# Where TensorE's sums over the states stand in a scan step: ahead of the step's middle third or behind it

## The chip, the core and the metric

The kernel runs on one core of a Trainium2 chip, as one program. The metric is the time of one execution on the device in microseconds. The core's engines run at the same time, each from a queue of its own that it works through in order: TensorE (PE in the profile) multiplies matrices, VectorE (DVE) does elementwise work, reductions and scans, ScalarE (ACT) activations and copies, GpSimd (POOL) a few copies and the indirect transfers, and SyncE (SP) starts most transfers between the device's memory and the core's.

## The reference

The reference is one decoder layer in float32 over 8 sequences of 512 tokens with 512 features: a state-space block (Mamba), cross attention, and a layer of 32 experts, with a layer norm behind each. The part that the change touches is the scan of the first block:

```python
dt = jax.nn.softplus(dt @ dt_proj_w + dt_proj_b)
dA = jnp.exp(A[None, None] * dt[..., None])
dBx = dt[..., None] * B_ssm[:, :, None, :] * x_main[..., None]

def scan_fn(h, inp):
    dA_t, dBx_t, C_t = inp
    h = dA_t * h + dBx_t
    y_t = jnp.einsum('bdn,bn->bd', h, C_t)
    return (h, y_t)
...
y = y + x_main * D_param[None, None, :]
y = y * jax.nn.silu(z)
out = res_scale * (y @ out_proj_w) + residual
```

There are 1024 channels with 16 states each. `einsum('bdn,bn->bd')` is the sum over the states: the states `h` times `C`, added up over the 16 states of a channel.

## The kernel before

The kernel has three phases: `layers` (scan, attention, router and the shared expert), `experts` and `finish`. Only `layers` matters here. It goes over 16 chunks: 8 sequences of two halves with 256 tokens each. A chunk has 32 steps, `k` = 0 to 31, one for each of four quarters `q` of the channels, four groups `g` of the states, and two halves `jj` of a quarter. A step works on a tile `h` of 128 partitions (32 channels with 4 states each) by 4 by 257 values. There are six such tiles in turn (L487).

One step, in the order in which the source emits it:

- `steps_in` (L494, VectorE) multiplies the repeated `dt*x` (tile `rep`) by `B` (tile `bc`) into `h`. In a step with `k` mod 8 = 1, `gated` (L535, VectorE) also multiplies the finished `py` of the quarter before into `zs`.
- the first third of the step's parts;
- `scan` (L501, VectorE) runs the recurrence over `h` with the decays `l_da`;
- for the next step, `carry` (L488, ScalarE) takes a new `h` and puts the old state into it, and `decays` (L480, ScalarE) forms its exponentials in one of two tiles `l_da`; then `keep` (L506, ScalarE) saves the state of the step before;
- the middle third of the parts;
- the sums over the states of the pair of steps before, if there are any: `products` (L519 and L521, TensorE);
- `collect` (L510, VectorE) multiplies `h` by `C`, and every second step it makes the next `products`;
- the last third of the parts.

`products` of the steps `k` = 2p and 2p + 1 is made at the end of step 2p + 1 and emitted in step 2p + 2, so it is emitted in even steps. Four matmuls, one for each 32 rows of the accumulator `py` in PSUM, add up the states of both `h` of the pair with the constant `fold`; at the first group of a quarter one more (L519) starts `py` with `x*D`. There is one `py`. In the profile each of these matmuls counts as two instructions. When they are done, both `h` are free again.

The "parts" are everything else that has to go on beside the scan. `part` puts them on a list, and the list is split into thirds by place (L1154 to L1156): the rest of the chunk's own projection (`gate_x` and `convolve`, L343 in the profile, 16 instructions each), `prepare` (L437: the `dt` of the next quarter), `back` (L552: the projection out, in two calls of 16 instructions, followed by `norm`, L561), and, by a budget of weights, the units of the attention of the sequence before (`units`) and the keys and values of the next one (`sources`; their matmuls are L756). In the attention `maximum` (L819 on TensorE, then L821 on VectorE) finds the largest score, `negate` (L828) turns the four maxima of a pair of heads into rows, `weigh` (L845, then L849 on ScalarE) takes the exponentials of the scores, and `gather` (L861) multiplies them by the values. One budget covers two chunks: an even chunk begins with the next sequence's keys and values and comes to the attention near its step 18; the odd chunk behind it ends the attention near its step 15 and then does the router and the shared expert. The chunks 0 and 1 have no attention, since there is no sequence before them.

In which third a part lands follows from how many there are: of one part it is the middle third, of two none is in the middle, of three one, of four two, of five one. So at `k` = 2 the middle third of a chunk without other work is `back`, at `k` = 4 `gate_x`; in the last even steps of an even chunk and the first of an odd one it is, for example, `weigh` and `gather`, or `weigh`, `gather` and `negate`.

The order of the source is not yet the order in an engine's queue: a scheduler between the two lays out the queues, and it can let an instruction that is ready pass one that is not. The waits between the engines, and for a free buffer, are then made from the data that instructions share.

Of the kernel before, what the change touches and what calls it, by code (L numbers as in the profile page):

```python
# [89 lines left out]
def layers(ctx, tc, a, x1d, filld, based, xbuf, arm):  # L90
# [203 lines left out]
    def settle(force=False):  # L294

        due, later = [], []
        for x in left:
            (due if force or not clock or x[0] <= clock[0] else later).append(x)
        for _, part in due:
            rest = part()  # L300
            if rest:
                later.append(rest if isinstance(rest, tuple) else (0, rest))
        left[:] = later
        return due
# [107 lines left out]
    def bcast(f, g):  # L412

        got = []
        for r0 in (g, NST + g):
            t = bcp.tile([P, T], F32, tag="bc", name="bc")
            src = f["scr"].rearrange("(n s g) t -> n g s t", n=2, s=NQ)[r0 // NST, r0 % NST]
            nc.sync.dma_start(t, src.unsqueeze(0).to_broadcast([QP, NQ, T]))
            got.append(t.unsqueeze(1).to_broadcast([P, NB, T]))
        f["bc", g] = got  # L420
# [63 lines left out]
    def carry(t, q, g, jj):  # L484

        last = state[:, q, g, jj].unsqueeze(2)
        h = mp.tile([P, NB, T + 1], F32, tag="h", name="h", bufs=6)  # L487
        nc.scalar.copy(h[:, :, 0:1], last if t else nothing)  # L488
        return h
# [217 lines left out]
    def sources(b):  # L707

        st, todo = {}, []

        def begin():
            load("Wv")
            st["cT"] = cT = quad("s2", "cT")
            nc.sync.dma_start(cT, rows(a["ctx"][b]))
            st["mk"] = mk = p1.tile([P, S], U8, tag="mk", name="mk")
            nc.sync.dma_start(mk, a["mask"][b : b + 1, :].to_broadcast([P, S]))
            kept[b] = [dp.tile([S, D], F32, tag="vd", name="vd"), dp.tile([D, S], F32, tag="kd", name="kd")]

        def values(pc):
            if pc == 0:  # L720
                load("Wk")
            w, cT = loaded["Wv"], st["cT"]
            ps = dense(lambda dc: cT[:, dc, pc * P : (pc + 1) * P], lambda dc: w[:, dc, :])

            def put():
                v = p3.tile([P, D], F32, tag="row", name="v")
                nc.scalar.copy(v, ps)
                nc.sync.dma_start(kept[b][0][pc * P : (pc + 1) * P, :], v)

            return put  # L730

        def keys(oc):
            if oc == 0 and b:
                load("Wq")
            w, cT = loaded["Wk"], st["cT"]
            ps = dense(lambda dc: w[:, dc, oc * P : (oc + 1) * P], lambda dc: cT[:, dc, :])

            def put():

                k = p3.tile([P, D], F32, tag="row", name="k")  # L740
                nc.vector.scalar_tensor_tensor(k, ps, bk[:, oc : oc + 1], st["mk"], ALU.add, ALU.mult)
                nc.sync.dma_start(kept[b][1][oc * P : (oc + 1) * P, :], k)

            return put

        todo.append((0, begin, False))
        for j in range(SC):
            todo.append((3.4, lambda j=j: values(j), False))
        for j in range(DC):
            todo.append((3.4, lambda j=j: keys(j), False))  # L750
        return todo
# [307 lines left out]
    def do(fn, *args, first=False):  # L1059

        if first:
            dry(False)
        rest = fn(*args)
        settle()
        if rest:
            left.append(rest if isinstance(rest, tuple) else (0, rest))
# [6 lines left out]
    def work(k):  # L1073

        front = 6.9 if k in (2, 3) else 3.4 if 4 <= k < 8 or k in (12, 14, 17, 20, 23) else 1.0 if k in (11, 25) else 0.0
        return 1.2 + front
# [24 lines left out]
    ahead, products = carry(0, 0, 0, 0), None  # L1101
# [3 lines left out]
    for i, (b, t) in enumerate(chunks):  # L1105
        nf = {}
        after = chunks[i + 1] if i + 1 < len(chunks) else None
        if t == 0:
            side, spent = units(b - 1) if b else sources(0), 0.0

            own = [work(k) for k in range(len(steps))] * 2
            whole = sum(own) + sum(x[0] for x in side)
        for k, (q, g, jj) in enumerate(steps):
            if i and k == 1:
                bcast(f, NG - 1)
            if after and 28 <= k < 31:
                bcast(nf, k - 28)
            qf, nq = (f, q + 1) if q + 1 < CC // 2 else (nf, 0)
            h = ahead

            parts = []

            def part(fn, *args, first=False):
                parts.append((do, fn, *args, first))

            if k in (2, 3) and old:
                part(back, k - 2, *old)
            if 4 <= k < 8:
                part(gate_x, k - 4, f)
            if k == 8:  # L1130
                parts.append((finish_silu, f["zs"]))
            if k % 8 == 0 and q + 1 < CC // 2:
                part(prepare, q + 1, f)
            if k == 25 and after:
                part(prepare, 0, nf)
            if after:
                if k == 8:
                    part(norm_x, nf)
                if k == 11:
                    for j in range(DC // 2):  # L1140
                        part(flip_x, j, nf)
                if k in (12, 14, 17, 20):
                    part(convolve, after[1], (12, 14, 17, 20).index(k), nf, first=(k == 12))
                if k == 22:
                    parts.append((finish_silu, *nf["xs"].values()))
                if k == 23:
                    part(x_proj, nf)
            if side and (k >= 4 or t and k < 2):
                at = t * len(steps) + k + 1
                while side and spent + sum(own[:at]) <= whole * at / len(own):  # L1150
                    w, fn, alone = side.pop(0)
                    spent += w
                    part(fn, first=alone)
            thirds = [[], [], []]  # L1154
            for m, x in enumerate(parts):
                thirds[round((m + 0.5) * 3 / len(parts) - 0.5) if x[0] is do else 1].append(x)  # L1156

            def run(m):
                clock[0] += 1
                settle()  # L1160
                for x in thirds[m]:
                    if x[0] is do:
                        do(*x[1:-1], first=x[-1])
                    else:
                        x[0](*x[1:])

            steps_in(f, q, g, jj, h)
            more = qf is f or after
            if k % 8 == 6 and more:
                repeat(qf, nq, 0, 1)  # L1170
            if k % 8 == 1:
                if k > 1:
                    gated(q - 1, f)
                elif old:
                    gated(CC // 2 - 1, old[2])
            if i == 0 and k == 0:
                load("Wo")
            if i == 0 and k == 2:
                biases()
            if k == 0 and old:  # L1180
                twice_x(*old)
            if k == 5 and after:
                load_x(*after, nf)
            run(0)
            scan(das[n % 2], h)
            n += 1

            if k + 1 < len(steps) or after:
                then = steps[(k + 1) % len(steps)]
                ahead = carry(t if k + 1 < len(steps) else after[1], *then)  # L1190
                decays(f if k + 1 < len(steps) else nf, *then, das[n % 2])
                if k % 8 == 5 and more:
                    repeat(qf, nq, 0, 0)
                    repeat(qf, nq, 1, 0)
                if k % 8 == 6 and more:
                    repeat(qf, nq, 1, 1)
            if held:
                keep(*held)
            held = t, q, g, jj, h
            run(1)  # L1200

            if products:
                products()
            products = collect(f, q, g, jj, h)
            run(2)
            while i < 2 and cleared < E * (i * len(steps) + k - 6) // (2 * len(steps) - 7):
                clear(cleared)
                cleared += 1
        while t and side:
            _, fn, alone = side.pop(0)  # L1210
            do(fn, first=alone)
        old = (b, t, f)
        f = nf
# [435 lines left out]
```

## Time and profile before

Three runs took 5262.2, 5269.8 and 5275.3 us; the median is 5269.8 us.

| what | us |
| --- | --- |
| the profiled execution | 5265.2 |
| its span, first to last instruction | 5263.4 |
| PE busy | 4483.6 (85%) |
| DVE busy | 4170.1 (79%) |
| ACT busy | 2584.7 (49%) |
| `scan` L501, 512 of 2.29 | 1165.1 |
| `collect` L510, 512 of 1.22 | 618.6 |
| `steps_in` L494, 512 of 1.22 | 613.9 |
| sums L521, 2048 instructions | 370.8 |
| sums L519, 128 instructions | 77.6 |
| ACT's `carry` (L488) waiting for the sums, 74 times | 111.3 |
| PE waiting for the maximum L821 at L819, 94 times | 139.4 |
| PE waiting for the maximum L821 at `negate` (L828), 34 times | 74.8 |

A line of a group gives the line of the code, the engine, the operation and its tiles; then, behind a bar, the time that the group was busy and the mean duration of one in ns; then, behind another bar, how long the engine was idle just before these instructions, and what ended most of that. A line of a timeline has the start, the busy time and the instruction; `x2` says that two equal neighbours were merged, and the bracket gives the idle time before and what ended it. PE's four matmuls of one sum run beside each other on 32 columns each, so eight instructions of some 0.6 us take 1.06 us together.

### The profile page before, as it was taken

The page shows a single profiled execution, that of the slowest core. Times are in us where ns is not written, and L with a number is a line of the kernel's source. Part 1 is how long each engine was busy: PE and PEld are TensorE (multiplying, and loading weights), DVE is VectorE, ACT ScalarE, POOL GpSimd, SP SyncE. Part 2 cuts the span into 40 slices and gives each one's busy share as a digit, 9 for nine tenths or more (in the row PEclk, how much of TensorE's full clock was granted, in tenths as well). Part 3 has the DMA queues.
Part 4 walks back from the last instruction along what each step waited for, and adds up shares of the span by engine and source line. Part 5 has one row for each costly group of instructions (what it writes and reads, how often), then busy time and mean ns, then how long its engine had stood idle before and what let it go on. Part 6 is the DMA issues. An engine that isn't in the chain of part 4 may idle for free. (4 is left out here: it accounts for less than half of the span.)

```text
span 5263.4 us, 54340 instructions
## 1 busy us (share of the span) xinstructions
PE 4483.6 (85%) x17184; PEld 2454.6 (47%) x17184; DVE 4170.1 (79%) x5333; ACT 2584.7 (49%) x5765; POOL 587.0 (11%) x426
## 2 busy tenths in 40 slices
PE   6768879888888988888898888878899999999895
PEld 3324234333423423343342343333478888877775
DVE  7999898989989998998999899883356666655555
ACT  5566565655556556565656656543222333323233
POOL 1000002001100200200020020010112111111111
PEclk8879999999998999999898999989899999999998
DMA  8885345435634634543473454433244444444344
GB/s 236 265 231 156 74 118 175 116 97 135 180 83 104 200 95 107 161 142 97 95 217 74 120 176 116 107 106 106 96 116 134 133 126 134 134 124 126 116 125 157
DMA packets 486437, 711.62 MB, mean 135 GB/s; under 512 B 121576, under 2 KB 205064, under 8 KB 483952
## 3 DMA queue, kind: packets, MB, share of 16 engines
q1 hardware_dynamic: 449984, 626.90, 41.8%
q0 software_dynamic: 33280, 67.81, 5.8%
q10 hardware_dynamic: 2736, 11.54, 0.5%
q8 instruction: 220, 3.60, 0.3%
q14 instruction: 217, 1.78, 0.1%
HBM read 391.24 MB, written 164.79 MB: 106 GB/s over the span
## 5 line engine op out<-in xcount | busy, mean ns | idle before, releaser
L480 ACT ACTIVATE l_da<-rep,l_aneg 128x256 f32<-128x256 f32 x2048 | 893.4, 499 | 948.1 <-DVE h L501 884.5
L501 DVE TENSOR_TENSOR_SCAN h<-l_da,h 128x1028 f32<-128x1028 f32 x512 | 1165.1, 2290 | 20.9 <-ACT l_da L480 18.3
L494 DVE TENSOR_TENSOR h<-rep,bc 128x1024 f32<-128x1024 f32 x512 | 613.9, 1216 | 107.7 <-PE py L521 90.7
L510 DVE TENSOR_TENSOR h<-h,bc 128x1024 f32<-128x1024 f32 x512 | 618.6, 1215 | 2.0
L521 PE MATMUL py<-h,l_fold 128*32 128x512 f32 x2048 | 370.8, 647 | 110.1 <-DVE h L510 92.3
L819 PE MATMUL ps_s<-l_ka,l_qa 64*128 64x512 f32 x1024 | 329.2, 714 | 139.8 <-DVE mx L821 139.4
L1334 PE MATMUL ps_h<-xT,w 128*128 128x224 f32 (+3 forms) x1536 | 376.4, 395 | 36.8 <-issue 29.7
L1427 POOL DMA_INDIRECT based<-y,xe x160 | 272.8, 1705 | 1157.8 <-ACT y L1406 432.4
L821 DVE TENSOR_REDUCE mx<-ps_s 128x2 f32<-128x1024 f32 x256 | 310.0, 1216 | 66.5 <-PE ps_s L819 66.2
L861 PE MATMUL po<-eT,l_va 128*64 128x512 f32 x1024 | 303.6, 674 | 47.5 <-ACT eT L849 42.9
L1334 PEld LDWEIGHTS ps_h<-xT,w 128*128 128x128 f32 x1536 | 293.3, 192 | 100.3 <-issue 41.6
L845 PE MATMUL ps_t<-l_qa,l_ka 64*128 64x512 f32 x1024 | 306.0, 669 | 23.9 <-ACT eT L849 23.3
L849 ACT ACTIVATE eT<-ps_t 128x1024 f32<-128x1024 f32 x256 | 258.7, 1015 | 128.7 <-PE ps_t L845 128.5
L694 POOL DMA_INDIRECT xbuf<-x2t,dest x128 | 217.2, 1697 | 863.2 <-DVE dest L679 762.4
L343 PE MATMUL ps_z<-xnT,wm 128*128 128x256 f32 x1024 | 237.7, 388 | 28.7 <-DVE o L561 23.7
L756 PE MATMUL ps_p<-x2T,wa 128*128 128x512 f32 x512 | 242.0, 627 | 20.5 <-ACT hT L950 13.8
L552 PE MATMUL po<-wm,zs 128*128 128x512 f32 x512 | 246.7, 636 | 13.4 <-DVE z L963 11.7
L1334 PE MATMUL ps_h<-t,s 128*128 128x224 f32 (+3 forms) x1024 | 247.4, 392 | 5.8 <-DVE hT L1355 5.8
L343 PE MATMUL ps_x<-xnT,wm 128*128 128x256 f32 x1024 | 245.6, 392 | 4.9 <-ACT xnT L332 2.8
L1355 DVE TENSOR_TENSOR hT<-ps_h,p 128x224 f32<-128x224 f32 (+3 forms) x128 | 55.3, 432 | 242.7 <-PE ps_h L1334 242.7
L343 PEld LDWEIGHTS ps_z<-xnT,wm 128*128 128x128 f32 x1024 | 194.9, 193 | 90.5 <-DVE o L561 37.0
L343 PEld LDWEIGHTS ps_x<-xnT,wm 128*128 128x128 f32 x1024 | 195.5, 195 | 81.6 <-issue 44.8
(239 smaller groups left out, 6971.3 us busy)
## 6 DMA issues: line engine op xcount, KB each, us to landing
w<-in_w SPq DMA_DIRECT2D x93, 1024.0 KB
wm<-in_in_proj_w SPq DMA_DIRECT2D x128, 512.0 KB
rep<-dt SPq DMA_DIRECT2D x256, 256.0 KB
rep<-dtx SPq DMA_DIRECT2D x256, 256.0 KB
xbuf<-zero SPq DMA_DIRECT2D x32, 1362.5 KB
xe<-xbuf SPq DMA_DIRECT2D x32, 1362.5 KB
wm<-in_out_proj_w SPq DMA_DIRECT2D x64, 512.0 KB
wa<-in_sw SPq DMA_DIRECT2D x24, 1024.0 KB
```

The costliest lines, as they stand in the source:

```text
L343: nc.tensor.matmul(ps[:, i, :], w[:, dc, i * P : (i + 1) * P], f["xnT"][:, dc, :], start=(dc == 0), stop=(dc == DC - 1),)
L480: nc.scalar.activation(da[:, n, 1:], dt[:, j, i, :], AF.Exp, scale=aneg[:, 2 * q + i, 2 * jj + j, g : g + 1])
L494: nc.vector.tensor_tensor(h[:, :, 1:], dtx.rearrange("p j i t -> p (j i) t"), f["bc", g][0], ALU.mult)
L501: nc.vector.tensor_tensor_scan(flat, da.rearrange("p n t -> p (n t)"), flat, 0.0, ALU.mult, ALU.add)
L510: nc.vector.tensor_tensor(h[:, :, 0:T], h[:, :, 1:], f["bc", g][1], ALU.mult)
L521: nc.tensor.matmul(f["py"][j * QP : (j + 1) * QP, :, :], fold, hs[j // 2][:, 2 * (j % 2) : 2 * (j % 2) + 2, 0:T], start=False, stop=g == N ...
L819: nc.tensor.matmul(ps[:, j, :], qa[r, lt * P : (lt + 1) * P], ka[r, :], start=True, stop=True)
L821: return lambda: nc.vector.tensor_reduce(mx[:, lt, :].unsqueeze(2), ps, AX.X, ALU.max) and None
L845: nc.tensor.matmul(ps[:, j, :], ka[r, kc * P : (kc + 1) * P], qa[r, :], start=True, stop=True)
L861: nc.tensor.matmul(po[j * 2 * HD : (j + 1) * 2 * HD, :], va[:, kc, i, j * HD : (j + 2) * HD], eT[:, j, :], start=(kc == 0), stop=(kc == SC ...
L1334: nc.tensor.matmul(ps, w[:, n, r * P : (r + 1) * P], x[:, n, 0:cols], start=not more and n == 0, stop=n == 1, skip_group_check=more,)
L1427: put = nc.gpsimd.indirect_dma_start(out=based, out_offset=bass.IndirectOffsetOnAxis(ap=xe.bitcast(I32)[:, j, D + E :], axis=0), in_=ys[j] ...
```

## The change

The sums of the pair before are emitted directly behind the next scan and what ScalarE does for the step, and the middle third of the parts comes behind them. The sums themselves, the parts, and how these are split into thirds stay as they were.

```diff
             if held:
                 keep(*held)
             held = t, q, g, jj, h
-            run(1)
-
             if products:
                 products()
+            run(1)
+
             products = collect(f, q, g, jj, h)
             run(2)
```

## The prediction

> **What bounds the kernel now.** I read the table by stretches first, then the groups by line, then the waits, and last the timelines of VectorE (DVE) and TensorE (PE).
>
> By stretches (start:end, length, then busy time of each engine, granted clock and DMA):
>
> ```profile
> 820.00:1000.00 180.00, 158.09 (x535) 73.39 (x533) 166.19 (x180) 101.54 (x245) 38.10 (x21) 0.97 0.61 178
> 1000.00:1097.00 97.00, 77.13 (x298) 23.44 (x298) 85.68 (x71) 54.83 (x120) 0.00 (x0) 0.89 0.28 62
> 1097.00:1139.00 42.00, 39.83 (x152) 20.95 (x150) 35.83 (x39) 17.95 (x44) 0.00 (x0) 0.98 0.55 166
> 820.00:1275.00 455.00, 382.20 (x1383) 165.61 (x1381) 411.56 (x452) 267.05 (x595) 41.24 (x29) 0.94 0.47 129
> ```
>
> The last line is two chunks, one batch. DVE is busy 411.6 of 455 us (90%), PE 382.2 (84%). Neither covers the batch alone: in the attention (1000 to 1097) DVE idles 11.3 us and PE 19.9, in turns; from 1097 to 1139 PE is all but full (39.8 of 42). The experts start near 3500 us and are not touched.
>
> The groups on the path, from the page, and DVE's wait on the sums from the list of waits:
>
> ```profile
> L494 DVE TENSOR_TENSOR h<-rep,bc 128x1024 f32<-128x1024 f32 x512 | 613.9, 1216 | 107.7 <-PE py L521 90.7
> L521 PE MATMUL py<-h,l_fold 128*32 128x512 f32 x2048 | 370.8, 647 | 110.1 <-DVE h L510 92.3
> ```
>
> ```profile
> DVE h L494 <- PE py L521: 90.7, 38, 6.8
> ```
>
> So 38 times `steps_in` (L494) waited for the sums (L521) to give back a buffer of `h`. There are six buffers, three pairs of steps, and L494 of one pair waits for the sums of the pair three before it. The sums stand far back in PE's queue: near 1505 us they run 35 us after the `collect` that they need. The reverse wait, sums for collect, is 92.3 us, and 60.2 of it lie before 350 us.
>
> Where the 90.7 us are, DVE and PE of one batch:
>
> ```profile
> 1053.05 2.36 DVE L494 TENSOR_TENSOR h<-rep,bc 128x1024 f32<-128x1024 f32 x2 [2.54 <-PE py L521]
> ...
> 1069.36 2.36 DVE L494 TENSOR_TENSOR h<-rep,bc 128x1024 f32<-128x1024 f32 x2 [3.28 <-PE py L521]
> ...
> 1107.24 2.36 DVE L494 TENSOR_TENSOR h<-rep,bc 128x1024 f32<-128x1024 f32 x2 [5.42 <-PE py L521]
> ```
>
> ```profile
> 1063.25 0.27 PE L828 MATMUL ps_m<-l_ident,mx 128*2 128x128 f32 x1 [3.23 <-DVE mx L821]
> 1063.46 1.35 PE L819 MATMUL ps_s<-l_ka,l_qa 64*128 64x512 f32 x4
> 1064.41 2.02 PE L845 MATMUL ps_t<-l_qa,l_ka 64*128 64x512 f32 x4
> 1066.36 1.97 PE L861 MATMUL po<-eT,l_va 128*64 128x512 f32 x4
> 1068.26 1.07 PE L521 MATMUL py<-h,l_fold 128*32 128x512 f32 x8
> ```
>
> ```profile
> 1097.56 7.78 PE L552 MATMUL po<-wm,zs 128*128 128x512 f32 x16
> 1105.18 1.02 PE L519 MATMUL py<-xs,l_ident 128*128 128x512 f32 x2
> 1106.13 1.06 PE L521 MATMUL py<-h,l_fold 128*32 128x512 f32 x8
> ...
> 1115.83 3.72 PE L343 MATMUL ps_z<-xnT,wm 128*128 128x256 f32 x16 [1.56 <-DVE o L561]
> ```
>
> At 1053 to 1069 there is a ring: the sums free `h`, DVE runs two L494 (2.36 us), a maximum (1.22), two scans (4.48), a collect (1.20) and a maximum (1.22); PE, which idled 3.23 us for that maximum, runs `negate`, `maximum`, `weigh`, `gather`, and only then the next sums. The round took 16.3 us (1053.05 to 1069.36), and the middle third of that step is `weigh` and `gather`: they stand between the transposes and the sums.
>
> **The change part by part.** Nothing is added or removed; the 256 groups of sums (8 matmuls, 1.06 us; every fourth with two of L519, 1.02 us) move ahead of the middle third of an even step. They issue no DMA. What they pass, by which part falls in that third: `weigh`, `gather`, `negate`, some `maximum` (about 1.1 us each), `gate_x` and `convolve` (3.7 us), `back` (7.8 us), `prepare` (1.1 us), and in others nothing on PE. SP's queue keeps its issues; the loads that such a part starts are only issued behind it as before. POOL's and ACT's work is not passed, only PE's.
>
> Source order is not queue order: two L494 stand ahead of two scans at 1053, though each step writes L494, scan, collect. At 1139 `negate` ran ahead of a `gather` written before it. So not-ready work was overtaken when the queues were laid out, and I expect a sum to pass a ready part only where its collects are done by that layout's time.
>
> Now the waits of L494, read one by one from DVE's timeline in the seven odd chunks that carry attention (3 to 15).
> - Step 0: 1.10, 2.54, 2.67, 2.48, 2.64, 1.18, 1.09, in all 13.7 us. The sums pass `weigh` and `gather`, 1.92 + 1.22 = 3.1 us at 1049 to 1052: more than any of the waits. All 13.7 go.
> - Step 2: 2.35, 3.28, 3.17, 3.22, 3.19, 3.22, 3.15, in all 21.6 us. They pass 2.02 + 1.97 = 4.0 us: all 21.6 go. By the ring: 16.3 less 4.0 is 12.3 us, less than DVE's own work in it, 12.5 us (16.3 less its idle 3.28 and 0.53), so DVE then sets the pace.
> - The last quarter of the even chunk, step 28: seven times 1.29, 9.0 us. They pass one `gather` at 1.0 us: 7.0 go.
> - Step 6: 6.82, 5.42, 5.34, 5.36, 5.35, 5.36, 5.34, in all 39.0 us. The sums pass `back` (7.8 us), so this wait too ends. But PE works without a break from 1097.56 to 1114, and `norm` (L561) waits for the end of both `back` calls, which is the same in either order. What DVE gains it mostly spends waiting for L561. What remains is the 1.56 us that PE idles for L561 ahead of `gate_x`, into which the next sums (1.06) now fall. I take 7 x 1.06 = 7.4; the bounds are 0 and 39.0.
> - The other seven or so waits, 90.7 - 13.7 - 21.6 - 9.0 - 39.0 = 7.4 us: at step 20 the middle third has no PE work. Nothing goes.
>
> The cost: what is passed comes 1.06 us later. In PE's slack that is free: 19.9 us per batch in the attention, and in the first chunks PE waits for DVE anyway. It is not free for `prepare` at step 8 of an even chunk, which stands right ahead of its sums (901.99, then 903.05) and for which DVE waits 3.10 us (L457 at 913.34). There 7 x 1.07 = 7.5 us are lost. If PE's slack were gone, each of the 197 even steps that have PE work in their middle third would cost up to 1.06 us; bounds 0 and 209, and I take the 7.5, near the lower, since the table by stretches shows 84% for PE.
>
> Sum: -13.7 - 21.6 - 7.0 - 7.4 + 7.5 = -42.2 us. The profiled span of 5263.4 becomes 5221; with the 1.8 us around it (5265.2 - 5263.4) 5223. That execution was 4.6 us under the median shown (5269.8), so **5228 us**.
>
> A rule on the clock bears on the ring. In the rows, after 3.23 us of idling `weigh` and `gather` took 2.02 and 1.97 us; after the 0.66 us idle ahead of the next round they took 1.02 and 1.08. The Trainium skill, "TensorE: Matmul & The Clock Gate" (The HAM clock gate), says an idle window of about 3.4 us halves the clock and about as long a busy one restores it. By it, idling cut from 3.2 to under 1 us would also give back the 1.8 us of each round; that lies within the waits counted above, so the sum is not changed.
>
> A rule against the change: "PSUM — Partial Sum Buffer" (Engine vs sequencer instructions) says matmuls start and complete in program order. The row agrees: PE idled 92.3 us at L521 for collects, nothing passing. By the rule alone every late sum now also holds the part it has passed; what that would make is the third rival.
>
> **The rivals.**
> - *The waits only move.* The freed DVE meets the maximum's scores (L821 waits 66.2 us for L819 now) or `rep` (the decays wait 53.7 us) instead. For it: step 6 is just such a case. Against: in the ring DVE's and PE's work both fit in 14 us. It gives nothing back but the 7.5 lost at most: about 5270.
> - *All of it comes.* If `norm` does not hold DVE at step 6, 90.7 us go: 5269.8 - 90.7 = 5179. Against: PE's full stretch.
> - *PE is held in order* (the slower side). Place: chunks 0 to 2, where DVE is behind PE. There nine even steps per chunk have `prepare`, `back`, `gate_x` or `convolve` in the middle third. If the sums are queued ahead of these though their collects are late, PE stands for the mean wait seen there, 60.2 / 17 = 3.5 us, with 1 to 8 us of work behind it. 27 x 3.5 = 95 us, of which DVE feels what delays `convolve` and `prepare`. It decides from 12 of the 27 on, when it eats the 42 us. In full: 5270 + 95 - 42 = 5323; half: 5275 to 5290. For it: the 92.3 us and the strict order. Against: the layout overtakes late work, and in these chunks PE has room.
>
> **How the numbers follow.** The forecast 0.48, all of it 0.10, the waits only move 0.17, PE held 0.25. What this kernel's measurement can tell from no change is 0.3%, 16 us: the forecast and "all of it" are faster, 0.58; the moved waits are the same, 0.17; PE held is slower, 0.25. The forecast's own range is 5190 (most of step 6 too) to 5250 (half of the ring). With the rivals 5180 to 5295: the low end takes most of the 90.7, the high end the half-held case and a little more.
>
> **What would show it.** L494's wait for PE falls from 90.7 us to 30 or less, with none over 4 us at step 2; `weigh` and `gather` near 1064 to 1068 stand behind the sums; PE's wait for the maximum (139.4 us, and 74.8 at `negate`) shrinks; the batch's period falls from 455 us by about 6. Wrong: L494's wait goes and DVE's idle time at L821, L457 or L561 grows as much; or PE's wait at L521 for L510 rises well over 92 us before 700 us, and the first two chunks get longer.

## The result and the profile after

| kernel | median us | lowest to highest | runs |
| --- | --- | --- | --- |
| before | 5266.0 | 5260.5 to 5275.3 | 4 |
| after | 5311.6 | 5305.5 to 5318.1 | 4 |

The ratio is 1.0089, with a 95% interval of 1.0077 to 1.0102: the change made the kernel 46 us slower, where 42 us less were forecast. The profiled execution took 5316.9 us, with a span of 5315.2.

The two groups that the change is about, from the page of after:

```profile
L494 DVE TENSOR_TENSOR h<-rep,bc 128x1024 f32<-128x1024 f32 x512 | 612.0, 1213 | 77.8 <-PE py L521 59.5
L521 PE MATMUL py<-h,l_fold 128*32 128x512 f32 x2048 | 396.5, 668 | 109.8 <-DVE h L510 96.4
```

VectorE's (DVE's) list of waits of after (who waits for whom: total us, times, longest):

```profile
DVE mx L821 <- PE ps_s L819: 139.2, 67, 10.2
DVE h L494 <- PE py L521: 59.5, 32, 3.5
...
DVE st L62 <- DMA xt<-in_x: 39.3, 7, 6.0
...
DVE o L561 <- PE po L552: 31.3, 8, 12.0
```

And TensorE's (PE's):

```profile
PE ps_t L845 <- DVE mx L821: 40.4, 7, 5.8
...
PE ps_z L343 <- ACT v L727: 15.2, 6, 3.4
```

The wait that the change aimed at did fall, 90.7 to 59.5 us. Other waits more than took its place: the maximum waits for its scores (L821, 66.2 to 139.2), the first operation on the next chunk's input for its load (L62, 5.7 to 39.3), `norm` for `back` (L561, 11.3 to 31.3); on PE two waits are new, 40.4 us at L845 (before 0.5) and 15.2 at L343 for ScalarE's (ACT's) copy L727 (before none).

**Where the 46 us are.** I took the start of every scan in both traces and subtracted the lengths of the same step pairs (pair 6 is the time from the scan of step 6 to that of step 8). The first two chunks are 1.5 us longer in all. In chunks 2 to 15 the steps 6 to 11 of the even chunks lose 48.5 us (8.5, 26.6 and 13.4 by pair). In the odd chunks step 4 gains 18.9 and step 6 gives back 11.6, and the pairs 10 and 12 go by -58.4 and +76.9, a net loss of 18.5. Not all of this stays: the steps 12 to 17 of the even chunks give 10.5 back, and over all their steps the even chunks lose 37.6 us and the odd ones 9.5. The even chunks are read best from the table by stretches, taken from the scan of step 2 to that of step 12 of the chunks 4 to 14, six rows for each kernel (the first and the sum are shown; the columns are start:end, length, busy time of PE, its weight loads, DVE, ACT and POOL, PE's granted clock, DMA share, GB/s). Before:

```profile
846.50:916.30 69.80, 63.84 (x213) 31.04 (x211) 58.92 (x65) 38.37 (x96) 21.20 (x12) 0.98 0.71 225
...
sum 417.10, PE 383.60 PEld 186.51 DVE 353.71 ACT 230.36 POOL 127.38; mean PE 63.93 PEld 31.09 DVE 58.95 ACT 38.39 POOL 21.23
```

After:

```profile
853.00:928.00 75.00, 66.99 (x216) 32.36 (x216) 58.73 (x66) 39.22 (x98) 18.30 (x11) 0.93 0.65 206
...
sum 463.70, PE 404.98 PEld 193.34 DVE 352.66 ACT 235.12 POOL 134.35; mean PE 67.50 PEld 32.22 DVE 58.78 ACT 39.19 POOL 22.39
```

These stretches alone are 46.6 us longer. PE was busy in 92% of them before: it is the engine nearest to its limit there, though over a batch it has 16% to spare. DVE's work is the same. PE's idle time grew by 25.2 us (46.6 - 21.4), and its busy time by 21.4, for nearly the same number of matmuls (216 against 213 in the row shown), at a granted clock of 0.91 to 0.96 where it had 0.98.

**What happens there**, in chunk 4. In the even chunk's step 4 the sums pass one block of `values` (L756, 3.7 us), `h` comes free earlier, and the layout of DVE's queue now has inputs and scans ready while `norm` goes through its five short dependent operations, L74 to L79. It puts them between. DVE's timeline before:

```profile
882.94 0.16 DVE L74 TENSOR_TENSOR m<-v,r 128x2 f32<-128x2 f32 x1 [3.23 <-ACT r L70]
...
883.73 0.16 DVE L79 SCALAR_TENSOR_TENSOR less<-mv,r 128x2 f32<-128x2 f32 x1
```

After:

```profile
889.13 0.16 DVE L74 TENSOR_TENSOR m<-v,r 128x2 f32<-128x2 f32 x1 [3.23 <-ACT r L70]
889.24 1.23 DVE L494 TENSOR_TENSOR h<-rep,bc 128x1024 f32<-128x1024 f32 x1
...
891.81 2.29 DVE L501 TENSOR_TENSOR_SCAN h<-l_da,h 128x1028 f32<-128x1028 f32 x1
894.02 0.13 DVE L77 TENSOR_TENSOR r<-r,m 128x2 f32<-128x2 f32 x1
894.07 2.29 DVE L501 TENSOR_TENSOR_SCAN h<-l_da,h 128x1028 f32<-128x1028 f32 x1
896.28 0.13 DVE L79 SCALAR_TENSOR_TENSOR less<-mv,r 128x2 f32<-128x2 f32 x1
...
904.33 1.29 DVE L62 BATCH_NORM_STATS2 st<-xt 128x6 f32<-128x512 f32 x2 [5.64 <-DMA xt<-in_x]
```

From the start of L74 to that of L79 it is 7.15 us instead of 0.79. ACT waits for L79, and what stands behind that wait is late too. ACT's timeline after:

```profile
894.13 1.30 ACT L480 ACTIVATE l_da<-rep,l_aneg 128x256 f32<-128x256 f32 x3 [3.69 <-DVE h L501]
896.45 1.52 ACT L81 ACTIVATE o<-o,less,r 128x512 f32<-128x512 f32 x2 [1.01 <-DVE less L79]
897.88 0.49 ACT L480 ACTIVATE l_da<-rep,l_aneg 128x256 f32<-128x256 f32 x1
898.27 0.56 ACT L727 COPY v<-ps_p 128x512 f32<-128x512 f32 x1
```

ACT's first wait, 3.69 us, is for a scan that gives the decays their buffer back. The wait for L79 and the two L81 behind it then put 2.5 us more (1.01 + 1.52) ahead of the copy L727. L727 empties the PSUM bank of a `values` block whose matmuls ended near 893.2 (in the kernel before this copy ran at 888.86), and PE waits for it ahead of the third `gate_x`. PE's timeline before:

```profile
886.91 7.07 PE L343 MATMUL ps_z<-xnT,wm 128*128 128x256 f32 x32
```

After:

```profile
893.10 3.62 PE L343 MATMUL ps_z<-xnT,wm 128*128 128x256 f32 x16
898.89 5.41 PE L343 MATMUL ps_z<-xnT,wm 128*128 128x256 f32 x16 [2.18 <-ACT v L727]
```

Before, these 32 matmuls ran in one piece of 7.07 us. Now PE waits 2.18 us, and the sixteen behind the wait take 5.41 us instead of 3.62: 4 us in a stretch where PE has little to spare.

### The profile page after: what moved, and what is told of

It is laid out like the page before. It is cut to its first block, busy times and chain, and to the rows that moved or that the text cites. A ratio compares the mean times of both kernels' runs of the same rounds, so it can differ in the third digit from the quotient of the medians.

```text
span 5315.2 us, 54319 instructions
## 1 busy us (share of the span) xinstructions
PE 4541.0 (85%) x17184; PEld 2467.2 (46%) x17184; DVE 4160.0 (78%) x5333; ACT 2595.7 (49%) x5765; POOL 599.0 (11%) x426
## 5 line engine op out<-in xcount | busy, mean ns | idle before, releaser
L494 DVE TENSOR_TENSOR h<-rep,bc 128x1024 f32<-128x1024 f32 x512 | 612.0, 1213 | 77.8 <-PE py L521 59.5
L510 DVE TENSOR_TENSOR h<-h,bc 128x1024 f32<-128x1024 f32 x512 | 616.2, 1214 | 1.8
L521 PE MATMUL py<-h,l_fold 128*32 128x512 f32 x2048 | 396.5, 668 | 109.8 <-DVE h L510 96.4
L819 PE MATMUL ps_s<-l_ka,l_qa 64*128 64x512 f32 x1024 | 348.3, 719 | 164.4 <-DVE mx L821 164.3
L821 DVE TENSOR_REDUCE mx<-ps_s 128x2 f32<-128x1024 f32 x256 | 309.6, 1214 | 139.3 <-PE ps_s L819 139.2
L845 PE MATMUL ps_t<-l_qa,l_ka 64*128 64x512 f32 x1024 | 325.3, 690 | 54.1 <-DVE mx L821 40.4
L861 PE MATMUL po<-eT,l_va 128*64 128x512 f32 x1024 | 298.3, 663 | 30.4 <-ACT eT L849 23.4
L343 PE MATMUL ps_z<-xnT,wm 128*128 128x256 f32 x1024 | 239.1, 390 | 25.2 <-ACT v L727 15.2
L819 PEld LDWEIGHTS ps_s<-l_ka,l_qa 64*128 64x128 f32 x1024 | 95.4, 206 | 353.3 <-DVE mx L821 268.9
L756 PE MATMUL ps_p<-x2T,wa 128*128 128x512 f32 x512 | 241.4, 626 | 18.4 <-ACT hT L950 12.5
L552 PE MATMUL po<-wm,zs 128*128 128x512 f32 x512 | 235.2, 613 | 24.0 <-DVE z L963 20.2
L343 PE MATMUL ps_x<-xnT,wm 128*128 128x256 f32 x1024 | 248.5, 396 | 7.1 <-ACT xp L363 6.1
L343 PEld LDWEIGHTS ps_x<-xnT,wm 128*128 128x128 f32 x1024 | 198.5, 198 | 82.1 <-issue 40.9
```

Of the source, the lines that this page charges most:

```text
L343: nc.tensor.matmul(ps[:, i, :], w[:, dc, i * P : (i + 1) * P], f["xnT"][:, dc, :], start=(dc == 0), stop=(dc == DC - 1),)
L494: nc.vector.tensor_tensor(h[:, :, 1:], dtx.rearrange("p j i t -> p (j i) t"), f["bc", g][0], ALU.mult)
L510: nc.vector.tensor_tensor(h[:, :, 0:T], h[:, :, 1:], f["bc", g][1], ALU.mult)
L521: nc.tensor.matmul(f["py"][j * QP : (j + 1) * QP, :, :], fold, hs[j // 2][:, 2 * (j % 2) : 2 * (j % 2) + 2, 0:T], start=False, stop=g == N ...
L819: nc.tensor.matmul(ps[:, j, :], qa[r, lt * P : (lt + 1) * P], ka[r, :], start=True, stop=True)
L821: return lambda: nc.vector.tensor_reduce(mx[:, lt, :].unsqueeze(2), ps, AX.X, ALU.max) and None
```

## The experiments

All keep the computation. "Early" is the changed place of the sums, "late" that of the kernel before. In e1, e2, e3 and e15 one condition chooses, with `i` the chunk and `k` the step:

```diff
+            early = bool(products and CONDITION) and (products() or True)
             run(1)
-            if products:
+            if products and not early:
                 products()
```

Most of the others lay one instruction behind another in its engine's queue (`tc.issue_after`); nothing else about the instruction changes.

| kernel | median us | ratio to before | interval |
| --- | --- | --- | --- |
| e1_all_but_step4 | 5279.8 | 1.0029 | 1.0018 to 1.0041 |
| e2_step4_alone | 5287.4 | 1.0041 | 1.0028 to 1.0053 |
| e3_attention_alone | 5266.2 | 1.0001 | 0.9992 to 1.0010 |
| e4_norm_held | 5305.0 | 1.0076 | 1.0061 to 1.0091 |
| e6a_maximum_spread | 5229.9 | 0.9931 | 0.9918 to 0.9945 |
| e6b_maximum_first | 5255.5 | 0.9988 | 0.9978 to 0.9997 |
| e8_own_buffer | 5320.8 | 1.0112 | 1.0096 to 1.0128 |
| e8c_own_buffer_before | 5272.0 | 1.0014 | 1.0004 to 1.0023 |
| e9_spread_alone | 5238.2 | 0.9934 | 0.9922 to 0.9947 |
| e10_copies_first | 5291.9 | 1.0045 | 1.0033 to 1.0057 |
| e11_step4_copies_first | 5286.7 | 1.0039 | 1.0026 to 1.0052 |
| e12_step4_norm_whole | 5272.1 | 1.0018 | 1.0009 to 1.0027 |
| e13_norm_whole | 5288.5 | 1.0052 | 1.0033 to 1.0071 |
| e14_norm_whole_spread | 5260.7 | 0.9992 | 0.9984 to 1.0001 |
| e15_two_places_back | 5248.2 | 0.9974 | 0.9965 to 0.9984 |
| e16_two_places_back_spread | 5220.6 | 0.9923 | 0.9909 to 0.9936 |

The kernel before, run beside them, had medians from 5262.7 to 5270.0 us; so ratios are compared, not medians.

### Which steps lose

```diff
+ e1: CONDITION = not (i % 2 == 0 and k == 4)
+ e2: CONDITION = (i % 2 == 0 and k == 4)
```

> The sums are early as in the changed kernel, except those of step 4 of every even chunk, which stay behind the middle third there (one group of 16 per even chunk, 8 groups of 256). Theory (norm torn apart): with step 4's sums early, h is free early, and VectorE's queue is laid out with two L494 and two scans between the five small operations of norm (L74 to L79), so o is stored and xt loaded some 7 us late; steps 6 to 10 of the even chunks 4 to 14 cost 48 us in all. Then this kernel gives back 35 to 50 of the 46 us: 5262 to 5277, VectorE's wait at L62 for xt under 10 us. Rival (the new waits are spread: VectorE waits for the scores at L821, 87 us against 13): still 5300 to 5312.

> The kernel before, with the sums early at step 4 of every even chunk alone. Theory (norm torn apart): this one move makes nearly all of the loss: 5300 to 5315, VectorE waiting 30 us or more at L62 for xt, L494's wait for the sums as before (80 to 91 us). Rival (spread): 7 groups of 256 moved, within 5 us of before, about 5266 to 5271.

Taking one of the 32 sums of a batch back (e1) returns 0.0089 - 0.0029 = 0.6%, 32 of the 46 us; that one alone (e2) costs 0.41%, 22 us. Both times lie between the two ranges that were expected: the place is right in both directions, but it is not nearly all of the loss. That it costs less alone than its return brings, by 10 us, is within the intervals. A second place was then read from the profiles, the pairs 10 and 12 of odd chunks. PE's timeline of after, chunk 5:

```profile
1143.65 0.49 PE L828 MATMUL ps_m<-l_ident,mx 128*2 128x128 f32 x3
1149.94 2.08 PE L845 MATMUL ps_t<-l_qa,l_ka 64*128 64x512 f32 x4 [5.80 <-DVE mx L821]
```

and DVE's:

```profile
1146.48 2.29 DVE L501 TENSOR_TENSOR_SCAN h<-l_da,h 128x1028 f32<-128x1028 f32 x1
1148.69 1.20 DVE L821 TENSOR_REDUCE mx<-ps_s 128x2 f32<-128x1024 f32 x1
```

`negate` has done three of its four transposes, and the maximum for the fourth stands behind two inputs (L494, at 1143.50 and 1144.70) and a scan that DVE took first: 5.8 us in each of seven odd chunks, the 40.4 of the list of waits. The longest wait for a maximum at `negate` was 3.4 us before.

```diff
+ e15: CONDITION = not (i % 2 == 0 and k == 4 or i % 2 and 8 <= k <= 12)
```

> The changed kernel, with the sums behind the middle third again at step 4 of even chunks and at steps 8, 10 and 12 of odd chunks, early everywhere else. Theory (these two places are the loss, and the rest of the change is worth about nothing): 5255 to 5268. Rival (the loss is spread, e1's 15 us over the kernel before stand in other steps too): 5272 to 5285.

It came out under both ranges, 0.9974: with four of the 32 sums of a batch left late, the change gains 14 us. So the two places hold more than the whole loss, some 60 us. PE's wait of 40.4 us at L845 is not in e15's list. That the order of the maximum is what costs at the second place is read from the traces; no run held that order alone.

### What the waits at the attention's steps are worth

```diff
+ e3: CONDITION = i > 1 and (k >= 24 if i % 2 == 0 else k < 4)
```

> The kernel before, with the sums early only where the attention runs: steps 24 to 30 of the even chunks and 0 and 2 of the odd ones, from chunk 2 on. My forecast's mechanism alone (the ring of sums, steps_in, maximum, transposes): waits of L494 at steps 28, 0 and 2 are gone, about 6 us per batch, 5225 to 5240. Rival (the waits only move, to L821 for the scores): 5260 to 5272, with L494's wait lower and L821's wait for the scores higher by as much.

No change, 1.0001: the rival's range. This is the forecast for the steps 28, 0 and 2 alone, without the lossy steps, and nothing of it reaches the time. DVE's waits in e3:

```profile
DVE mx L821 <- PE ps_s L819: 108.1, 52, 11.6
...
DVE o L561 <- PE po L552: 30.2, 8, 11.1
...
DVE h L494 <- PE py L521: 16.8, 26, 1.2
```

L494's wait fell by 73.9 us; L821's rose by 41.9 and L561's by 18.9. One part of how it comes back is in DVE's timeline of e3,

```profile
1051.08 4.48 DVE L501 TENSOR_TENSOR_SCAN h<-l_da,h 128x1028 f32<-128x1028 f32 x2
1055.48 1.20 DVE L821 TENSOR_REDUCE mx<-ps_s 128x2 f32<-128x1024 f32 x1
```

and in PE's:

```profile
1056.73 2.08 PE L819 MATMUL ps_s<-l_ka,l_qa 64*128 64x512 f32 x4 [5.21 <-DVE mx L821]
1058.60 1.92 PE L845 MATMUL ps_t<-l_qa,l_ka 64*128 64x512 f32 x4
```

Before, this maximum ran at 1055.3, ahead of both scans. With `h` free earlier the scans are ready first, and the maximum is laid behind them. PE waits 5.21 us for it and then needs 2.08 and 1.92 us for what takes 1.13 and 1.02 when it comes without such a wait. From the scan of step 0 to that of step 2 it is now 15.85 us (1051.08 to 1066.93), against 16.31 before (1056.46 to 1072.77): half a microsecond gained where the forecast had 4.0.

The larger part comes back at `norm`. Counted from the scan of step 24 of the even chunk, the scans of the seven odd chunks are together 26.1 us ahead of the kernel before at step 4 and 45.0 at step 6, but 13.1 at step 8. Between the two stands L561, which waits for `back`. DVE and PE of e3, chunk 5:

```profile
1111.32 0.75 DVE L561 SCALAR_TENSOR_TENSOR o<-po,l_rs,o 128x512 f32<-128x512 f32 x1 [2.96 <-PE po L552]
```

```profile
1098.99 14.00 PE L552 MATMUL po<-wm,zs 128*128 128x512 f32 x32
```

The scan of step 6 starts 7.9 us earlier than before (1101.62, before 1109.51), but `back` ends only 1.3 us earlier (1112.99, before 1114.26). Up to the last scan e3's profile is 8.0 us shorter than that of the kernel before, and 9.2 us longer behind it, where no sum was moved; one profile of each can't tell whether this is more than scatter, and the eleven runs of e3 say 1.0001.

The next three ask whether a better order would let the saving through: e6a and e6b are e3 with the scans of odd chunks laid behind maxima, e9 is the same as e6a without moving any sum.

```diff
-        return lambda: nc.vector.tensor_reduce(mx[:, lt, :]...) and None
+        return lambda: mxs.update({(i, lt): nc.vector.tensor_reduce(mx[:, lt, :]...).ins})
...
-            scan(das[n % 2], h)
+            with tc.issue_after(mxs.pop(AT.get(k))) if ... else ExitStack(): scan(das[n % 2], h)
...
+ e6a, e9: AT = {0: (4, 2), 1: (4, 3), 2: (5, 1), 3: (5, 2), 4: (6, 0)}
+ e6b:     AT = {0: (4, 2), 1: (4, 2), 2: (5, 1), 3: (5, 1), 4: (6, 0)}
```

> The kernel is e3_attention_alone (sums early only at steps 24 to 31 of even chunks and 0 to 3 of odd ones, which ran at the time of the kernel before) with one thing more: in every odd chunk from the third on, the scan of step 0 is laid behind the maximum of pair 4 row block 2 on VectorE, that of step 1 behind 4.3, 2 behind 5.1, 3 behind 5.2, 4 behind 6.0, so that no maximum stands behind two scans (4.4 us). Theory (the wait for the sums was really saved, and lost again because the layout then put both scans ahead of a maximum that TensorE needs): TensorE's 3.1 and 5.2 us waits for the maximum in each round go, the rounds stay at or under the 16.3 us of the kernel before, 2 to 4 us fall out of each of three rounds in 7 chunks: 5205 to 5240. Rival (waits only move: TensorE's row of scores, weights and gathers sets the round whatever VectorE's order): 5258 to 5275, with VectorE's wait at L821 still above 40 us.

> As e6a_maximum_spread, but both scans of steps 0 and 1 are laid behind maximum 4.2, those of 2 and 3 behind 5.1, that of 4 behind 6.0: the order that the kernel before has there (in, in, maximum, scan, scan). Theory as there: 5215 to 5250, somewhat behind e6a since two scans still stand together. Rival (waits only move): 5258 to 5275.

> Control for e6a_maximum_spread: the kernel before, sums where they were, with the five scans of odd chunks laid behind the maxima as in e6a. Theory (e6a's gain needs both: the sums early, so that VectorE's h buffers are free, and the maxima spread): the waits of L494 for the sums stay near 90 us, time 5252 to 5270. Rival (the order of the maxima is the whole gain, and the place of the sums does nothing): 5225 to 5245, with e6a.

e6a gained 0.69%, inside the theory's range, as if the saving had been let through. The control fells this: e9, in which no sum is moved, gains 0.66%. The order of the maxima is the gain, and the place of the sums adds nothing that can be told from zero. e6b, the order of the kernel before, stays within 0.12% of that kernel; it came out between its two ranges. DVE's waits in e6a,

```profile
DVE mx L821 <- PE ps_s L819: 69.0, 44, 11.1
...
DVE o L561 <- PE po L552: 31.9, 8, 11.3
DVE h L494 <- PE py L521: 23.4, 32, 2.0
```

and in e9:

```profile
DVE h L494 <- PE py L521: 65.4, 33, 5.5
...
DVE mx L821 <- PE ps_s L819: 52.1, 25, 10.1
...
DVE o L561 <- PE po L552: 10.7, 1, 10.7
```

The 42 us that e6a has less at L494 it has more at L821 and L561 (38.1 us), at the same time for the whole. Counted as above, e6a is 71.4 us ahead of the kernel before at step 6 of the odd chunks and 38.1 at step 8; e9 is ahead by 33.1 and 33.2. So the sums add 38 us up to step 6, and 5 are left behind L561. In its chunk 5 DVE reaches step 6, counted from the scan of step 2, 5.6 us earlier than in e9, and then waits 3.22 us at L561, where PE's second `back` call ends when it ended anyway.

### Why step 4 of the even chunks loses

The first theory was that the wait of L62 for `xt` (39.3 us) is the loss. `xt` and the residual `o` share one buffer, so the load waits for the store of `o`, which stands behind the torn `norm`. In e8 and e8c `o` has another buffer in even chunks, that of the attention's exponentials `eT`:

```diff
-        f["o"] = o = mp.tile([P, NT_, D], F32, tag="xt", name="o")
+        f["o"] = o = (mp if t == 0 else p2).tile([P, NT_, D], F32, tag="xt" if t == 0 else "eT", name="o")
```

> The changed kernel, but in even chunks the residual tile o has a buffer of its own (that of the exponentials eT, idle then), so that the load of the next chunk's xt no longer waits for o's store, and so not for the torn-apart normalisation. Theory (the loss is the wait of L62 for xt behind the torn normalisation, 39.3 us against 5.7): that wait falls under 5 us and the time to 5270 to 5290. Rival (the next link, ScalarE's exponentials of prepare or the sums, is as late, so that the wait turns up at L457, L535 or L821): 5300 to 5315.

> Control: the kernel before with the same buffer for o. The wait of L62 for xt was only 5.7 us there. Theory: 5256 to 5266. Rival (the earlier load lets the layout tear the other normalisation, of xt, or moves VectorE's order ahead of the sums): 5275 to 5295.

The wait fell to 4.6 us and the time did not: 1.0112, above both ranges and no better than after. L494 waits 73.3 us for the sums instead of 59.5, and in chunk 4 the 5.64 us at L62 are 6.64 us at step 10's input. PE still had its wait for L727, 15.7 us in all. So ending that wait is not enough. What it is worth e8 leaves open: the pairs 6 to 10 of the even chunks lose 29.8 us in it instead of 48.5, but the pairs 14 and 16 of the odd chunks lose 19.0 instead of 2.7, and from the last scan to the first matmul of the experts it is 10.7 us longer. The last of these is a price of the borrowed buffer: the control e8c is 10.0 us longer there than the kernel before. (e8c's time, 1.0014, was slightly above its expected range.)

e4 held `norm` whole on DVE: it laid the input that follows in program order behind L79.

```diff
+            (lasts.append if name in ("ln2",) else id)(nc.vector.scalar_tensor_tensor(less, ...).ins)
...
+            with tc.issue_after(lasts.pop()) if lasts else ExitStack(): steps_in(f, q, g, jj, h)
```

> The changed kernel, with the steps_in that follows in the source laid behind the last small operation of norm (L79), by an order of issue and no wait, so that no L494 or scan of that step comes between L74 and L79. Theory (norm torn apart): the store of o and the load of xt come back to their old place, steps 6 to 10 of the even chunks lose most of their 48 us: 5265 to 5285. Rival (spread): 5300 to 5312. If L494 held back costs VectorE more than it saves: over 5312.

It missed: 1.0076. The input that it caught was step 7's, which had stood ahead of `norm` before. `norm` was whole and early, but the loads of `rep` came later in SP's queue, close ahead of the store of `o` (issued from 881.11 instead of 877.05, the store at 885.01 and 885.47). From the store's issue to that of the load of `xt` it was 6.7 us, against 2.8 before, and over the run PE waited 31.3 us for the copy L389 at L756 instead of 6.7. The next two name the steps instead, 8 and 9, and so leave the queue of SP as it was:

```diff
+            with tc.issue_after(lasts["ln2"]) if i > 1 and i % 2 == 0 and k in (8, 9) and ... else ExitStack(): steps_in(f, q, g, jj, h)
...
+ e12: on e2
+ e13: on the changed kernel
```

> e2_step4_alone (the kernel before, with only the sums of step 4 of even chunks early: ratio 1.0041) with steps 8 and 9's inputs (L494) of even chunks laid behind the normalisation's last short operation (L79), which gives VectorE the order of the kernel before there, while TensorE still does the sums ahead of the values block. Theory (the torn normalisation is the cost): 5262 to 5272, TensorE's idle time in steps 2 to 12 of even chunks back from 62.5 to under 47 us, those steps from 505.7 to under 480 us. Rival (TensorE's own order is the cost): 5280 to 5292.

> The changed kernel with the inputs of steps 8 and 9 of even chunks laid behind L79 as in e12. Theory (torn normalisation): 5275 to 5290; what is left over the kernel before is steps 10 and 12 of odd chunks (18.5 us) and the maxima behind two scans. Rival (TensorE's own order): 5300 to 5315.

The sum of e12's stretches from step 2 to 12, as above:

```profile
sum 426.10, PE 388.04 PEld 188.61 DVE 354.92 ACT 231.19 POOL 127.48; mean PE 64.67 PEld 31.44 DVE 59.15 ACT 38.53 POOL 21.25
```

They are back to 426.1 us; e2 had 451.6, the kernel before 417.1. (e2 gives 10.6 us back in the steps 12 to 17, so the stretches alone show too much.) By the whole time e12 gives back 0.0041 - 0.0018 = 0.23%, 12 of 22 us, at the upper end of its range, and e13 0.37%, 19 of 46, within its range. So the torn `norm` is part of what this place loses (0.41% in e2, 0.60% by e1), shown with the sums left early; by the medians it is over half, but the intervals leave room for well under half as well as for nearly all. DVE's wait for `xt` went with it (4.6 us in both). What stays in e12 goes with PE's own order: its wait for L727 is 8.4 us in these stretches (none before), since PE now comes to the second `values` block sooner and ACT's copy does not. That this wait is the whole rest is not shown.

The third link, ACT's copy, was tried with `norm` left torn: L727 ahead of L81 and of the decays of two steps.

```diff
+                with top[0].issue_after(cps[-1]) if name == "ln2" and ... else ExitStack(): nc.scalar.activation(o, t, ...)
...
+                with tc.issue_after(cps[4 * (i // 2) + 1]) if ... and k in (9, 10) and ... else ExitStack(): decays(...)
```

> The changed kernel, but in even chunks ScalarE's copy of the second values block (L727), which frees a PSUM bank for TensorE's third gate projection, is laid ahead of the two L81 that wait for the torn normalisation, and ahead of the decays of steps 10 and 11. Theory (TensorE sets the time of steps 2 to 12 of even chunks: 63.9 of 69.5 us busy before; the torn normalisation holds ScalarE, ScalarE holds the bank, TensorE waits 2.2 us and then multiplies at a lower clock): TensorE's wait at L343 for v falls from 15.2 to under 4 us, the granted clock of these steps comes up from 0.91 to 0.96 or more, 5278 to 5295. Rival (the next copy, zs at L389, is then late instead: TensorE's wait for it rises from 17.7 to 30 us): 5300 to 5318.

> e2_step4_alone (the kernel before, with only the sums of step 4 of even chunks early: 24 us slower) with ScalarE's copy laid ahead as in e10_copies_first. Theory: the wait for v (5.1 us) goes, and part of the wait for zs (18.3 against 6.7 before) with it, since ScalarE is through its queue earlier: 5266 to 5280. Rival: as e2, 5283 to 5295.

e10 came out in its range (1.0045, 0.44% given back, though its runs spread from 5271 to 5304 us); the wait for L727 halved, 15.2 to 7.7, where under 4 was expected. Its profile is that of its fastest run, 21 us under the median. e11 missed: 1.0039, as e2. In it PE's waits for L727 and L389 fell from 23.4 to 7.4 us over the run, and in these stretches a wait of 17.4 us at L519 for `gated` (L535, 4.0 in e2) came in. `gated` waits for ACT's silu. DVE, ACT and PE are each just in time here, and freeing one link shows the next.

### Together

```diff
+ e14: e13 with the scans behind the maxima of e6a
+ e16: e15 with the scans behind the maxima of e6a
```

> e13 with the maxima spread between the scans of odd chunks as in e6a and e9: the whole change, with both of VectorE's orders held. If the change itself is worth something, it comes out under e9 (which has the maxima spread and the sums where they were): 5200 to 5230. If waits only move: 5238 to 5262, no better than e9, worse by what steps 10 and 12 of odd chunks lose.

> e15 (sums behind the middle third at step 4 of even chunks and 8, 10, 12 of odd ones, early elsewhere) with the maxima spread between the scans of odd chunks as in e9. If e15's and e9's gains add (-16 and -34 us): 5205 to 5225. If both are the same gain, TensorE getting its maxima and sums sooner in the same ring: 5228 to 5245, as e9.

e14, the whole change with both orders held, is 0.9992, and e9, without the change, 0.9934: the change still costs 0.58%. The second place is still in it; the pairs 10 and 12 of its odd chunks lose 25.2 us. e16 is the fastest of all, 0.9923. Its time lies in the range that was expected if the gains of e15 and e9 add, but its interval also holds e9's ratio, so what early sums add to spread maxima is not settled.

## Why the prediction was wrong

- **The view of the bound** failed first. PE's share was read over the batch, 84%, and over a stretch of 180 us that was 88%. From step 2 to 12 of the even chunks it is 92%, and there the sums pass a `values` block, which the prediction's list of what they pass does not name. It saw the full stretch in the odd chunks alone.
- **The cost** was sized as what passes on PE: 7.5 us for `prepare` at step 8 of the even chunks, with 0 and 209 as bounds. The neighbouring steps 6 to 11 lose 48.5 us and the steps 10 to 13 of the odd chunks 18.5, and the mechanism is another: `h` free earlier changes what the layout finds ready, so the queues of DVE and ACT are laid anew. The text said that source order is not queue order, and used it only for the sums, never for what the freed buffers let in.
- **Steps 0, 2 and 28, 42.3 us together**: the waits went, as forecast. The step that failed is "DVE then sets the pace": the round took 15.3 us after the change (1061.95 to 1077.22) where 12.3 were forecast. DVE had the time, but its queue put two scans, 4.48 us, ahead of the maximum that PE stands for. And what was gained up to step 6 (45.0 us in e3) was mostly spent at L561, waiting for `back`: the limit that the prediction named for step 6 held for these steps too. Where the order of the maxima was cured (e6a), the time gained was the same as without the sums (e9). By e3's interval the term was worth 5 us at most either way.
- **Step 6, 7.4 of 39.0 us**: the reason for taking little was right. DVE's gain is spent waiting for L561, 11.3 to 31.3 us. The idle time of PE that the rest was to fill, at L343 behind L561, went from 23.7 to 5.6 us. What that was worth no run isolates. From the scan of step 0 to that of step 8 the odd chunks are 17.4 us shorter than before in the changed kernel, and 11.4 in e15; in e3, which leaves the sums from step 4 on late, they are 1.3 shorter.
- **The clock.** The prediction's 1.8 us per round came from slow rows after 3.23 us of idling. That is less than the window that it cites; only the rows carry it, and the section on the hardware below has more of them.
- **The rivals.** "The waits only move" named L821 and is what e3, and e6a against e9, show for the attention; it was given 0.17. "PE is held in order" had the right sign in the wrong place: PE's wait at L521 for L510 rose only from 92.3 to 96.4 us over the run, and the first two chunks lost 1.5. The true slow case was not among the rivals.
- **What would show it** worked as a test: L494's wait at 59.5 instead of 30 or less, more at L821 and L561, and a batch (two chunks) that from chunk 2 to 14 went from 451.2 to 456.1 us on average instead of falling by 6.

Open is whether one sum really costs less alone (e2, 22 us) than its return brings (e1, 32 us), where the 14 us that e15 gains come from, and how the second place, the steps 8 to 12 of odd chunks, splits over its three sums: e15 moved them together.

## What to carry to other kernels

Freeing a buffer earlier is a change to every queue whose work that buffer let wait: where an order is laid out by readiness, look for short dependent operations and for the reductions that another engine stands for, since the long operations that become ready will be put ahead of them. Read the bound in the steps that the moved work passes, not over the period. Follow a saved wait to the next place where the engine waits for the same producer: here DVE's lead was spent there. And when a mend gains, run it without the change that it mends: here the mend was the gain.

## What the runs showed of the hardware

PE slows after shorter idle times than expected. In both profiles the granted clock before 3500 us is either 1.00 or 0.50, and it holds for multiples of 3.41 us. I cut the time at full clock into windows of that length and took PE's idle time in each (the ends of matmuls are modelled, so these times are not exact). With over 1.9 us idle, the next window was at half clock in 80 of 80 cases before the change and in 72 of 73 after it; with under 1.2 us in 3 of 678 and 7 of 677; between the two in 21 of 101 and 19 of 84. The Trainium skill, "TensorE: Matmul & The Clock Gate" (The HAM clock gate), puts it at an idle window of about 3.4 us. The length agrees with these rows, but in them a window that was idle for a little over half was enough. In chunk 4 of the changed kernel, the window behind PE's wait of 2.18 us (for L727) reads:

```profile
898.96:902.37 3.41, 3.41 (x8) 2.75 (x9) 0.00 (x0) 2.15 (x6) 0.00 (x0) 0.50 0.71 263
```

The clock, the third number from the right, is 0.50. So the wait of 2.18 us cost 4 us.
